# Six places for rows, loads ahead of stores, and later weights in the convolution part of an attention-and-convolution kernel

## The chip, the core and the metric

The kernel runs on one core of one Trainium2 chip. A core has a matrix engine (PE), a vector engine (DVE), a scalar engine (ACT), a general engine (POOL) and a sequencer for transfers and synchronisation (SP). Each runs its own list of instructions in order and waits for others by semaphores. PE reads its operands from the on-chip memory SBUF (128 partitions) and writes to a second on-chip memory, PSUM, from which ACT and DVE take results. Transfers between SBUF and device memory are issued by SP, POOL or ACT as instructions of their own and are carried out by 16 transfer engines that all of these queues share.

The metric is the time of one execution on the device, in microseconds (us); the median of three runs is used.

## What the kernel computes

The reference has two layers on an image batch of 2 x 256 channels x 64 x 64. The first is a full self-attention (8 heads of 32, 4096 positions) whose result is blended with the input by a mask. The second gates the channels, runs attention in 8 x 8 windows, and ends in two grouped 7 x 7 convolutions whose result gates the tensor:

```python
x = _L0_conv_ref(x, mask, Wq, ...)            # attention over all 4096 positions, mask blend
# layer 1
x = x * sigmoid(relu(xp @ ca_w1 + ca_b1) @ ca_w2 + ca_b2)
o = window_attention(x)                        # 8x8 windows, 4 heads of 64
x = x + o @ out_w + out_b
x = shuffle_channels(x, groups=4)
y = conv7x7(x, sa_w1, groups=64); y = relu(bn1(y + sa_b1))
y = conv7x7(y, sa_w2, groups=64); y = bn2(y + sa_b2)
return x * sigmoid(y)
```

All is float32. The change concerns the last three lines.

## The kernel before, in words

**The long part.** `pipeline` walks through 512 slots of the first attention (2 images, 8 chunks of 512 positions, 2 groups of heads, 32 blocks of keys; line 1232). Between the slots it runs the stages of layer 1 for chunks that are done (`stage`, line 766) and issues the transfers that build the convolution weights as band matrices in device memory (`bands`, line 340). The last step of a stage writes the chunk's rows into device memory at `x_s`, with padding (line 1024).

**The convolution part.** `convolve` (line 1038) is a generator. It starts near the end of the slots, runs interleaved with the last stages, and then alone. The 64 channel groups are cut into 16 units of 4 groups (`UG`, `NU`). A 7 x 7 convolution is done as 7 horizontal taps, with a band matrix over image rows for each; three overlapping blocks of rows (`BLOCKS`) cover an image. The work is a list of 26 items of (unit, images) (line 1033), numbered from 0:

- items 0 to 8: units 0 to 8 of image 0 (`EARLY` is 9), whose rows exist before image 1 is done;
- items 9 to 15: units 2 to 8 of image 1;
- items 16 to 21: units 9 to 14, both images at once;
- items 22 to 25: unit 15 of image 0, unit 15 of image 1, units 1 and 0 of image 1.

**One iteration** of the loop at line 1191, for item k: `conv1(k+1)` puts 56 matmuls of the next item on PE, and ACT applies the first activation (line 1102). `conv2(k)` puts 112 matmuls on PE (line 1118); ACT turns the two PSUM tiles into `z` by a tanh (line 1129) and a scaling (line 1135). `gate(k)` multiplies `z` by the rows on DVE (line 1146) and issues 12 stores for each image, four of every twelve on SP and eight on POOL (line 1148), other splits in the last two items. Then `load_rows` issues the load of later rows, and `load_w` that of a later weight, both on SP. All waiting is by semaphores on the tiles. SP, like every engine, goes through its list in order: a load behind a store whose `z` is not ready waits with it.

**Places.** Rows of early items go to four places in one tile, `room` (`early`, line 1042). Later items use four other places, `xcs`, each large enough for two images, made when image 1 is written (`more`, line 1172). Item k + 4 takes the place of item k, so its load is issued in iteration k. `z` has four buffers, one for each image of an item (line 1127). Weights sit in a ring of 8 buffers (`EB`): units 1 to 9 are loaded by iteration 4; from iteration 9 on each iteration loads one more, units 10 to 15 and then unit 1 again (lines 1053 and 1205). Unit 10 takes the buffer that unit 2 leaves with item 9. The first item that reads unit 10 is item 17.

Of the kernel before, what the change touches and what calls it, by code (L numbers as in the profile page):

```python
# [17 lines left out]
B, C, H, W = 2, 256, 64, 64  # L18
# [12 lines left out]
EB = 8  # L31
DN = 8
EARLY = 9
# [4 lines left out]
KS, PAD = 7, 3  # L38
# [19 lines left out]
def conv_seq_kernel(ctx: ExitStack, tc: tile.TileContext, a, out):  # L58
    nc = tc.nc
# [40 lines left out]
    for h in range(HEADS0):  # L100
        n, rows = (0, 32) if h < HG else (1 + (h - HG) // 2, 64)
        p = rows * (h % HG if h < HG else h % 2)
# [271 lines left out]
    with (  # L374
# [50 lines left out]
        for i, (b, c) in enumerate(chunks):  # L425
            load_chunk()
            x = xs0[i]
# [105 lines left out]
    def pipeline(arm, shifted, pools):  # L533
# [499 lines left out]
        items = [(u, (0,)) for u in range(EARLY)] + [(u, (1,)) for u in range(2, EARLY)]  # L1033
# [4 lines left out]
        def convolve():  # L1038
            nb = len(BLOCKS)


            early, xcs, ycs = [], [], []
            room = cpool.tile([P, ROOM], F32, tag="room", name=f"xe{arm}")
            room = room.rearrange("p (k n g w) -> p k n g w", k=4, n=nb, g=UG)
# [6 lines left out]
            xs, ws, ys = {}, {}, {}  # L1051

            weights = deque([*range(1, NU), 1])
            dst = out.rearrange("b (g i) r w -> b i r g w", i=4)

            def load_w(u):
                if u >= NU:
                    return
                n = 2 * 32 * UW
                if u == 0:  # L1060
                    t = cpool.tile([P, n], F32, tag="w0", name=f"w{arm}{u}")
                else:
                    t = ep.tile([P, HG, CH], F32, tag="e", name=f"w{arm}{u}")
                    t = t.rearrange("p h n -> p (h n)")[:, 0:n]
                nc.sync.dma_start(t, w_s[u])
                ws[u] = t

            def load_x(k):
                u, images = items[k]
                x = xs[k] = early[k % 4] if k < EARLY else xcs[k % 4]  # L1070
                for i, b in enumerate(images):
                    nc.sync.dma_start(
                        x[:, nb * i : nb * i + nb].rearrange("p n g w -> p n (g w)"),
                        x_s[b, :, :, UG * u : UG * u + UG, :].rearrange("n p g w -> p n (g w)"),
                    )

            def load_rows(k):

                while len(xs) < min(k + 1, len(items)) and (
                    staged or B - 1 not in items[len(xs)][1]  # L1080
                ):
                    load_x(len(xs))

            def conv1(k):
                if k >= len(items):
                    return
                u, images = items[k]
                n = nb * len(images)
                w = ws[u][:, 0 : 32 * UW].rearrange("p (m g d) -> p g d m", g=UG, d=KS)
                s = psum1(f"c1{arm}{k}")  # L1090
                for d in range(KS):
                    for j in range(4):
                        nc.tensor.matmul(  # L1093
                            s[32 * j : 32 * j + 32, 0 : n * W],
                            w[:, j, d, :],
                            xs[k][:, 0:n, j, d : d + W],
                            start=(d == 0),
                            stop=(d == KS - 1),
                        )
                y = ys[k] = ycs[k % 2]  # L1100
                nc.scalar.activation(
                    y[:, 0:n, PAD : PAD + W],
                    s[:, 0 : n * W].rearrange("p (n x) -> p n x", x=W),
                    AF.Relu,
                    bias=cbias1[:, u : u + 1],
                )

            def conv2(k):
                u, images = items[k]
                n = nb * len(images)  # L1110
                y = ys.pop(k)
                w = ws[u][:, 32 * UW :].rearrange("p (m d) -> p d m", d=KS)
                tiles = [psum2(f"c2{arm}{k}_{hh}") for hh in range(2)]
                for d in range(KS):
                    for j in range(4):
                        r = slice(32 * j, 32 * j + 32)
                        for o in HALVES:
                            nc.tensor.matmul(  # L1118
                                tiles[j // 2][o, j % 2, 0 : n * W],
                                w[r, d, o],  # L1120
                                y[r, 0:n, d : d + W],
                                start=(d == 0),
                                stop=(d == KS - 1),
                            )
                zs = []
                for m in range(len(images)):
                    z = pool.tile([P, 4, nb * W], F32, tag="z", name=f"z{arm}{k}_{m}", bufs=4)
                    for hh in range(2):
                        nc.scalar.activation(  # L1129
                            z[:, 2 * hh : 2 * hh + 2, :],  # L1130
                            tiles[hh][:, :, m * nb * W : (m + 1) * nb * W],
                            AF.Tanh,
                            scale=0.5,
                        )
                    nc.scalar.activation(z, z, AF.Copy, bias=0.25, scale=0.25)  # L1135
                    zs.append(z.rearrange("p j (n x) -> p j n x", x=W))
                while held:
                    held.popleft()()
                return zs

            def gate(k, zs):
                u, images = items[k]
                for m, b in enumerate(images):
                    z = zs[m]
                    x = xs[k][:, nb * m : nb * m + nb, :, PAD : PAD + W]
                    nc.vector.tensor_mul(z, z, x.rearrange("p n g x -> p g n x"))  # L1146

                    engines = (nc.gpsimd, nc.gpsimd, nc.sync)
                    if k == len(items) - 1:
                        engines = (nc.scalar, nc.sync)  # L1150
                    elif k == len(items) - 2:
                        engines = (nc.scalar, nc.sync, nc.sync)
                    stores = 0
                    for n, (x0, r0, r1) in enumerate(BLOCKS):
                        for i in range(4):
                            p = 32 * i + 1 - x0
                            stores += 1
                            args = (
                                dst[b, i, r0:r1, UG * u : UG * u + UG, :],
                                z[p + r0 : p + r1, :, n, :],  # L1160
                            )
                            eng = engines[stores % len(engines)]
                            if eng is nc.scalar:
                                held.append(lambda a=args: nc.scalar.dma_start(*a))
                            else:
                                eng.dma_start(*args)  # L1166
                if k == len(items) - 1:
                    while held:
                        held.popleft()()


            def more():
                if staged and not xcs:

                    for n in range(3):
                        t = ep.tile([P, HG, CH], F32, tag="sum", name=f"xl{arm}{n}", bufs=3)
                        t = t.rearrange("p h n -> p (h n)")[:, 0 : B * nb * UG * WP]
                        xcs.append(t.rearrange("p (n g w) -> p n g w", n=B * nb, g=UG, w=WP))
                    xcs.append(pool.tile([P, B * nb, UG, WP], F32, name=f"xl{arm}3"))
                    load_rows(EARLY)  # L1180
                return bool(xcs)

# [8 lines left out]
            for k, (u, images) in enumerate(items):  # L1191
                while len(xs) <= k + 1 < len(items):
                    if not more():
                        yield
                conv1(k + 1)
                yield
                more()
                z = conv2(k)
                yield
                more()  # L1200
                gate(k, z)
                if xcs or k + 4 < EARLY:
                    load_rows(min(len(xs) + (k >= EARLY - 1), k + 4))

                if weights and (weights[0] <= 1 + EB or k >= EARLY):
                    load_w(weights.popleft())

        def run_later():
# [150 lines left out]
```

## Time and profile before

| | |
|---|---|
| median of 3 runs | 2908.93 us (2906.93 to 2909.06) |
| the profiled execution | 2910.0 us, span 2908.0 us |
| PE busy | 2864.2 us, 98% of the span |
| ACT, DVE, POOL busy | 2455.7, 2435.1, 584.8 us |
| convolution part, last 26 items | from about 2688 us to the end of the span |
| 840 KB of rows for two images (two loads), 420 KB for one | 23 loads of later rows |
| 896 KB for one unit's weights | 17 loads |

A profile line of a group gives the engine, the line of the kernel, the operation, output and input by name, how often, and the busy time. A line of the timeline gives start, duration, engine, line and operation of a run of like instructions, and in brackets how long the engine stood idle ahead of it and what ended that; "issue" there means that nothing the profile records ended it. In a table of windows each engine's busy time and count is given by stretch, then the granted clock of PE as a share, the busy share of the 16 transfer engines, and GB/s.

### The profile page before, as it was taken

To read this page: it belongs to the slowest core of one execution; us is meant where nothing else is said; L and a number is where in the kernel's file an instruction comes from. 1 tells how busy PE (TensorE), PEld (TensorE's weight loads), DVE (VectorE), ACT (ScalarE), POOL (GpSimd) and SP (SyncE) were. 2 spreads that over 40 slices of the span, in tenths; PEclk is the share of its full clock that TensorE was granted. 3 is DMA by queue.
4 is the path that set the end of the run, shared out by engine and by line. 5 is a ranking of instruction groups with operands and counts; after the bars stand their busy time and mean duration, and the time that the engine had idled before them with its cause. 6 is when DMAs were issued, how large, how long until landed. Compare 5 with 4: busy or idle time off the path is not lost.

```text
span 2908.0 us, 85469 instructions
## 1 busy us (share of the span) xinstructions
PE 2864.2 (98%) x37002; PEld 828.2 (28%) x37002; DVE 2435.1 (84%) x1344; ACT 2455.7 (84%) x4145; POOL 584.8 (20%) x965
## 2 busy tenths in 40 slices
PE   9999999999999999999999999999999999999997
PEld 3551122222222222222222222222222222222665
DVE  4249999899999999999989999999999899999211
ACT  5569989898989898989989898989898898989433
POOL 8111111111111212121111111111212110000468
PEclk9999999999999999999999999999999999999999
DMA  8546533333353535353433324343535342242574
GB/s 253 210 162 189 149 86 86 88 83 87 72 95 76 105 80 105 75 95 86 85 93 80 85 70 95 80 98 76 106 79 94 85 85 78 67 115 85 142 221 105
DMA packets 243590, 305.66 MB, mean 105 GB/s; under 512 B 118768, under 2 KB 135348, under 8 KB 242948
## 3 DMA queue, kind: packets, MB, share of 16 engines
q1 hardware_dynamic: 197072, 230.83, 28.7%
q0 software_dynamic: 41360, 66.48, 12.7%
q8 instruction: 293, 4.80, 0.7%
q10 hardware_dynamic: 4772, 2.79, 0.4%
q14 instruction: 93, 0.76, 0.1%
HBM read 221.88 MB, written 66.39 MB: 99 GB/s over the span
## 4 chain that ended last, share of the span: by engine, by line
PE 89%; DMA 4%; POOL 3%; issue 1%; DVE 1%; ACT 1%; ACTq 0%; SPq 0%; DVEq 0%; POOLq 0%
PE sa L643 35%; PE ava L695 33%; PE qka L529 4%; PE hya L529 3%; POOL out_dram L1166 2%; PE vwa L529 2%; PE opa L529 2%; PE v L475 2%; PE q L438 1%; PE k L438 1%; PE c2a L1118 1%; PE c1a L1093 1%; DMA invs<-inva 1%; PE sca L882 1%; DMA folda<-suma 1%
## 5 line engine op out<-in xcount | busy, mean ns | idle before, releaser
L656 ACT ACTIVATE ea<-sa 128x512 f32<-128x512 f32 (+1 forms) x3072 | 2037.0, 746 | 50.1 <-PE sa L643 23.3
L643 PE MATMUL sa<-qa,ka 32*64 32x512 f32 x16384 | 1146.6, 613 | 1.5 <-ACT vst L483 1.2
L701 DVE TENSOR_TENSOR suma<-suma,ea 128x2048 f32<-128x2048 f32 x480 | 1096.2, 2284 | 5.7 <-ACT ea L656 0.5
L695 PE MATMUL ava<-ea,va 128*32 128x512 f32 x8192 | 1091.6, 605 | 1.0
L701 DVE TENSOR_TENSOR odda<-odda,ea 128x2048 f32<-128x2048 f32 x420 | 958.3, 2282 | 46.1 <-ACT ea L656 46.0
L673 POOL DMA_DIRECT2D folda<-suma x336 | 235.5, 891 | 1664.0 <-DVE suma L703 980.0
L643 PEld LDWEIGHTS sa<-qa,ka 32*64 32x64 f32 x16384 | 242.3, 129 | 786.0 <-ACT ea L656 716.9
L695 PEld LDWEIGHTS ava<-ea,va 128*32 128x32 f32 x8192 | 161.4, 108 | 834.2 <-issue 804.7
L1166 POOL DMA_DIRECT2D out_dram<-za x240 | 135.7, 573 | 51.7 <-DVE za L1146 26.6
L701 DVE TENSOR_TENSOR suma<-ea,ea 128x2048 f32<-128x2048 f32 x32 | 73.1, 2286 | 58.8 <-ACT ea L656 58.8
L529 PE MATMUL qka<-ua,qkv_w 128*32 128x512 f32 x1024 | 115.8, 592 | 0.1
L1146 DVE TENSOR_TENSOR za<-za,xla 128x768 f32<-128x768 f32 x23 | 22.1, 959 | 99.3 <-ACT za L1135 46.6
L785 ACT ACTIVATE ta<-hya,bf 128x512 f32<-128x512 f32 x32 | 20.3, 685 | 99.6 <-PE hya L529 93.6
L1024 POOL DMA_DIRECT2D xs<-xo x94 | 72.0, 1037 | 137.2 <-DVE xo L1009 133.3
L457 DVE TENSOR_REDUCE top<-sq 128x128 f32<-128x2048 f32 x16 | 36.6, 2284 | 74.5 <-ACT sq L451 74.5
L741 POOL DMA_DIRECT2D invs<-inva x62 | 34.2, 559 | 297.6 <-DVE inva L756 296.6
L1118 PE MATMUL c2a<-yca,wa 32*64 32x192 f32 (+1 forms) x2912 | 86.3, 368 | 5.5 <-issue 5.1
L903 ACT ACTIVATE ewa<-ewa,mxwa 128x64 f32<-128x64 f32 x256 | 85.4, 346 | 1.5 <-DVE mxwa L894 1.5
L1129 ACT ACTIVATE za<-c2a 128x384 f32<-128x384 f32 x64 | 27.9, 487 | 69.2 <-PE c2a L1118 37.7
L789 DVE TENSOR_TENSOR ta<-ta,mca 128x512 f32<-128x512 f32 x32 | 22.0, 688 | 65.7 <-ACT ta L785 65.7
L1118 PEld LDWEIGHTS c2a<-yca,wa 32*64 32x64 f32 x2912 | 68.1, 191 | 24.5 <-issue 17.3
L861 ACT ACTIVATE qka<-qka,qkv_b 128x512 f32<-128x512 f32 x64 | 40.3, 683 | 39.5 <-PE qka L529 39.5
(143 smaller groups left out, 1714.8 us busy)
## 6 DMA issues: line engine op xcount, KB each, us to landing
ka<-ks SPq DMA_DIRECT2D x256, 256.0 KB
va<-vs SPq DMA_DIRECT2D x256, 256.0 KB
wa<-ws SPq DMA_DIRECT2D x17, 896.0 KB
ws<-zeros SPq DMA_DIRECT2D x16, 896.0 KB
folda<-suma POOLq DMA_DIRECT2D x224, 64.0 KB, 3.1
folda<-suma POOLq DMA_DIRECT2D x112, 128.0 KB, 3.9
xs<-xo POOLq DMA_DIRECT2D x78, 140.0 KB, 7.7
xla<-xs SPq DMA_DIRECT2D x23, 420.0 KB
```

The source lines that it names most:

```text
L438: nc.tensor.matmul(s[:, g, :], w[:, kc, g * P : (g + 1) * P], rhs, start=(kc == 0), stop=(kc == KC - 1),)
L475: nc.tensor.matmul(sv[:, m, :], xs0[i][:, kc, m * P : (m + 1) * P], wv[:, kc, :], start=(kc == 0), stop=(kc == KC - 1),)
L529: nc.tensor.matmul(out[o : o + 32], weights[:, o : o + 32], x, start=start, stop=stop)
L643: nc.tensor.matmul(heads[j][o], k[r, cols][:, o], q[r, g, :], start=True, stop=not shifted)
L656: nc.scalar.activation(e[:, h, :], tile, AF.Exp, scale=SCALE0)
L673: nc.gpsimd.dma_start(dst[p : p + rows], total[rows * k : rows * k + rows, h, :], accum_op=ALU.add if k else ALU.bypass,)
L695: nc.tensor.matmul(av[r, :], v[:, m % PB, r], e[:, j, :], start=start, stop=stop)
L701: nc.vector.tensor_add(total, first.pop(m % chains, total), e)
L903: nc.scalar.activation(e[:, n, :], e[:, n, :], AF.Exp, bias=mx[:, n : n + 1], accum_out=rs[:, n : n + 1],)
L1024: eng.dma_start(x_s[b, n, p + r0 : p + r1].rearrange("r g w -> g r w"), xo[64 * h : 64 * h + 64, oc, r0 - WS * c : r1 - WS * c, :],)
L1118: nc.tensor.matmul(tiles[j // 2][o, j % 2, 0 : n * W], w[r, d, o], y[r, 0:n, d : d + W], start=(d == 0), stop=(d == KS - 1),)
L1166: eng.dma_start(*args)
```

## The change

Five edits in `convolve`:

1. `xcs` gets two more places, both in `room`, the tile of the early rows: first its second half, then its first half. The ring of later rows has six places and starts with item 9 at place 0; item k + 6 takes the place of item k.
2. `gate` is split: `gate(k)` holds only the multiplications of all images of the item, `store(k)` all its stores.
3. Between them stands `load_rows`, so that the loads of iteration k are ahead of its stores in SP's list, and it looks `len(xcs)` items ahead, six in place of four.
4. Stores of items with two images alternate between POOL and SP, 12 and 12 in place of 16 and 8. Item 23 (third from the end) puts 8 of its 12 on SP and 4 on POOL in place of 4 and 8. The last two items' splits are as before.
5. The weights of units 10 to 15 and the second load of unit 1 are loaded from iteration 13 on in place of 9.

```diff
-                x = xs[k] = early[k % 4] if k < EARLY else xcs[k % 4]
+                x = xs[k] = early[k % 4] if k < EARLY else xcs[(k - EARLY) % len(xcs)]
...
             def gate(k, zs):
                 u, images = items[k]
+                for m in range(len(images)):
+                    x = xs[k][:, nb * m : nb * m + nb, :, PAD : PAD + W]
+                    nc.vector.tensor_mul(zs[m], zs[m], x.rearrange("p n g x -> p g n x"))
+
+            def store(k, zs):
+                u, images = items[k]
+                engines = (nc.gpsimd, nc.gpsimd, nc.sync)
+                if k == len(items) - 1:
+                    engines = (nc.scalar, nc.sync)
+                elif k == len(items) - 2:
+                    engines = (nc.scalar, nc.sync, nc.sync)
+                elif k == len(items) - 3:
+                    engines = (nc.gpsimd, nc.sync, nc.sync)
+                elif len(images) == 2:
+                    engines = (nc.gpsimd, nc.sync)
+                stores = 0
                 for m, b in enumerate(images):
-                    z = zs[m]
-                    x = xs[k][:, nb * m : nb * m + nb, :, PAD : PAD + W]
-                    nc.vector.tensor_mul(z, z, x.rearrange("p n g x -> p g n x"))
-
-                    engines = (nc.gpsimd, nc.gpsimd, nc.sync)
-                    if k == len(items) - 1:
-                        engines = (nc.scalar, nc.sync)
-                    elif k == len(items) - 2:
-                        engines = (nc.scalar, nc.sync, nc.sync)
-                    stores = 0
                     for n, (x0, r0, r1) in enumerate(BLOCKS):
...
                     xcs.append(pool.tile([P, B * nb, UG, WP], F32, name=f"xl{arm}3"))
+                    for n in (2, 0):
+                        xcs.append(room[:, n : n + 2].rearrange("p k n g w -> p (k n) g w"))
                     load_rows(EARLY)
...
                 gate(k, z)
-                if xcs or k + 4 < EARLY:
-                    load_rows(min(len(xs) + (k >= EARLY - 1), k + 4))
-
-                if weights and (weights[0] <= 1 + EB or k >= EARLY):
+                if xcs:
+                    load_rows(min(len(xs) + (k >= EARLY - 1), k + len(xcs)))
+                elif k + 4 < EARLY:
+                    load_rows(k + 4)
+                store(k, z)
+
+                if weights and (weights[0] <= 1 + EB or k >= EARLY + 4):
                     load_w(weights.popleft())
```

More of the change, by code (lines that the diff above doesn't have):

```diff
@@ L1159, in gate @@
                                 dst[b, i, r0:r1, UG * u : UG * u + UG, :],
-                                z[p + r0 : p + r1, :, n, :],
+                                zs[m][p + r0 : p + r1, :, n, :],
                             )
```

## The prediction

> **What bounds the kernel now.** I read the page first, for the engine that sets the whole; then a table of windows over the convolution part, which alone is changed; then the timelines of PE and SP there, and POOL's at the end.
>
> ```profile
> PE 2864.2 (98%) x37002; PEld 828.2 (28%) x37002; DVE 2435.1 (84%) x1344; ACT 2455.7 (84%) x4145; POOL 584.8 (20%) x965
> ...
> q8 instruction: 293, 4.80, 0.7%
> ```
>
> PE bounds the whole. Its 74,004 matmuls and weight loads over the 293 transfers of the instruction queue are 253 apiece: this queue feeds PE its instructions, 4.80 MB / 293 = 16 KB at a time.
>
> ```profile
> 2762.00:2808.00 46.00, 40.86 (x1203) 33.81 (x1202) 6.71 (x7) 15.23 (x29) 32.79 (x59) 0.96 0.73 210
> 2808.00:2866.00 58.00, 57.99 (x1124) 33.70 (x1114) 9.59 (x10) 20.53 (x38) 44.99 (x81) 1.00 0.66 185
> 2866.00:2893.00 27.00, 25.50 (x784) 21.45 (x780) 6.71 (x7) 13.70 (x27) 26.51 (x48) 1.00 0.44 94
> ```
>
> The columns are the stretch, its length, busy time of PE, PE's weight loads, DVE, ACT and POOL, granted clock, transfer share, GB/s. PE idles 5.1 us in the one-image items (first row), nothing in the two-image items, 1.5 us in the last items. POOL is full at the end, with stores only.
>
> ```profile
> 2781.99 0.76 PE L1118 MATMUL c2a<-yca,wa 32*64 32x192 f32 x17 [1.17 <-issue]
> ...
> 2788.30 1.60 PE L1118 MATMUL c2a<-yca,wa 32*64 32x192 f32 x58 [1.56 <-issue]
> ...
> 2802.97 0.63 PE L1118 MATMUL c2a<-yca,wa 32*64 32x192 f32 x11 [2.18 <-issue]
> 2803.53 4.19 PE L1093 MATMUL c1a<-xla,wa 128*32 128x192 f32 x56
> ...
> 2884.39 2.54 PE L1093 MATMUL c1a<-xla,wa 128*32 128x192 f32 x56 [0.84 <-DMA xla<-xs]
> ```
>
> The large stalls are in the middle of a `conv2`, wait for no data, and end 2.3 to 2.4 us after a 16 KB transfer of the instruction queue starts (2779.58, 2786.01 and 2800.72 in the transfer records): PE waits for its own instructions. After the third, PE runs at half clock from about 2803 to 2807 and the next `conv1` takes 4.19 us in place of 2.5. The last line is the only stall on rows.
>
> ```profile
> 2785.45 2.25 SPq L1166 DMA_DIRECT2D out_dram<-za  x4
> 2787.75 0.38 SPq L1072 DMA_DIRECT2D xla<-xs  x1
> 2788.23 0.43 SPq L1065 DMA_DIRECT2D wa<-ws  x1
> ...
> 2868.71 4.19 SPq L1166 DMA_DIRECT2D out_dram<-za  x8
> ...
> 2879.83 1.42 SPq L1072 DMA_DIRECT2D xla<-xs  x1
> 2881.35 20.73 SPq L1166 DMA_DIRECT2D out_dram<-za  x22
> ```
>
> SP issues rows and a weight together, behind the stores. In the transfer records rows for one image take some 24 pieces of 60 ns on each engine, 1.4 us, a weight 8 pieces of 285 ns, 2.3 us. The last row load is issued at 2879.83 and used at 2884.39.
>
> [...] The trace shows 0.50 after 2.18 us and a row of shorter stalls.
>
> **The ideal and what is lost.** Unstalled durations in the timeline are 2.47 and 2.57 us for conv1 and conv2 of one image, 4.76 and 4.81 of two. From conv2(7), 2762.3, to the last matmul at 2892.6 are 130.3 us. Needed: conv1(9 to 25) 7 x 2.47 + 6 x 4.76 + 4 x 2.47 = 55.7; conv2(7 to 25) 9 x 2.57 + 6 x 4.81 + 4 x 2.57 = 62.3; 118.0 in all. Lost: 12.3. By place: conv2(7, 8) 0.6; conv2(10) to conv2(14) 1.6 + 2.1 + 0.5 + 0.4 + 2.7 + 1.7 + 0.6 = 9.6, of which the half clock is 2.2; the last items 1.9, with the late row's 0.84. After the last matmul come tanh, scaling, product, 24 stores by SP and ACT, landing: 15.4 us to the span's end.
>
> **The change, part by part.**
>
> *Two places, look-ahead of six.* No instruction is added. Item 25's rows are issued in iteration 19 in place of 21, about 17 us earlier: the 0.84 us wait goes, and row traffic leaves the last items. I take 1.0 us. Other rows were never awaited, so their earlier coming gives nothing itself. The places in `room` are free: item 13's needs item 6's product, item 14's needs item 8's, the last instruction before it.
>
> *Loads ahead of stores.* The loads pass the stores on SP only; POOL's list keeps its order. In items 0 to 4 too they wait for the same product as the stores did, so they come 1.6 us earlier and meet nothing new. A one-image store set waits behind 1 or 2 loads, 0.4 to 0.9 us on SP. Hidden: `z` returns four images later, some 20 us in one-image items, 16.5 us after the product in two-image ones; POOL's 12 x 0.57 = 6.8 us plus 3.5 us to land is 10.3. If it were not, ACT's tanh would wait, then PSUM, then PE. For two-image items all stores now wait for the second product, 1.6 us more, covered by the same slack.
>
> *Stores from POOL to SP.* Six items move 4 each, item 23 moves 4: 28 x 0.573 = 16.0 us off POOL, which ended at 2896.9, not last. On SP 28 x 0.50 (six runs of 8 in the two-image items: 24.2 us / 48) = 14.1 us more. In a two-image iteration SP then has 12 x 0.50 + a load 0.4 + a weight 0.4 = 6.8 of 9.57 us: room. At the end: items 20 to 25 have 12, 12, 4, 8, 8, 6 stores = 50 x 0.50 = 25 us from 2870.3, so SP is at leisure again before item 24's product (2892.2). I take 0.
>
> *Weights four iterations later.* The four weights of iterations 9 to 12, 4 x 2.3 = 9.2 us of transfer time, leave the one-image items; weights 10 and 11 are still issued there (iterations 13, 14), but most of their data moves under conv1(16) and conv1(17), which run at 4.76 us per 112 instructions and so need a block half as often. Against it, rows come denser: two loads in each of iterations 8 and 10 to 14. Transfer need per 5.0 us: 2 x 1.4 rows + 1.3 stores (0.30 share over 4.4 us per image near the end) = 4.1, where rows plus weight plus stores were 5.0 to 6.4. So the saturated stretch becomes a busy one[...]. Rows-only iterations before (items 9 to 11) cost 0.2, 0.35, 0 and once 1.6: mean 0.5 per iteration. Pairs of rows: bounded by 0.3 below (no worse than one) and 1.1 above (twice that mean); I take 0.7. After: iterations 5 to 9 five times 0.6 = 3.0, 10 to 13 four times 0.7 = 2.8, the half clock at a chance of one in seven 0.3: 6.1 in place of 0.6 + 9.6 = 10.2. Gain 4.1; at the bounds, nine times 0.3 or 1.1, it is 7.5 or 0.3.
>
> *Is weight 10 in time?* From iteration 13's product to conv1(17) are conv2(13)'s end + 2.47 + 2.57 + 4.76 + 2.57 = 12.4, less 2.8 to the product's end: 9.5 us. Two loads 0.9, four stores 1.7, and 5.2 to 6.9 us from issue to the last piece (weights of 2747 and 2809): 7.8 to 9.5, with 0.4 for the signal 8.2 to 9.9. I take 0 and keep a loss of 0.5 in the range. Weight 11 has 14 us.
>
> Sum: 4.1 + 1.0 = 5.1 us. The profiled execution's 2910.0 would become 2904.9; it stands 1.1 above the median, so 2908.9 - 5.1 = 2903.8.
>
> **Rivals.** *(B) Nearly all stalls go*, since without weights a fetch is never late enough, and the clock stays whole: 10.2 - 1.0 left + 1.0 late row = 10 us, 2899 (2897 to 2901). For: the two longest stalls have a weight in flight. Against: the 1.17 us stall at 2781 began before any. *(C) Paired rows stall PE as weights did*: gain -1 to 2.5, 2906.4 to 2910. For: the row bytes moved forward nearly equal the weight bytes moved back. Against: pieces a fifth as long. *(D) Slower: SP becomes the last queue.* Its 50 stores from 2870.3 would end later than 2902.1 once one costs over 0.64 us; beyond 0.2% of loss from about 0.75 us, at some 2915 to 2920. For: the last 14 took 9.84 us, 0.70 each. Against: 0.50 in the runs of 8, and gaps between products there. That the change doesn't take effect is no rival I can see: six places change the place of every item.
>
> **How the numbers follow.** 0.2% is 5.8 us, about what a measurement of this kernel can tell from no change: bounds 2903.1 and 2914.7. Main case 0.50, 2901.3 to 2906.4, of which 0.19 below 2903.1; B 0.22, C 0.20, D 0.08. Faster 0.19 + 0.22 = 0.41; same 0.31 + 0.20 = 0.51; slower 0.08. The range 2898.3 to 2910.0 leaves out D, some of B (0.07) and a little of C.
>
> **What would show it.** Right: conv2(11) to conv2(13) with stalls under 1 us, PE's clock 1.00 from 2762 to 2866, transfer share more even (near 0.75 in both), no idle on rows at conv1(25), POOL done before 2893, SP's tail about as before. Wrong: a stall at conv1(17) on weights; half clock again; SP's stores of item 21 still running when item 24's product is done; ACT's tanh waiting for stores while PE stands.

## The result

The changed kernel takes 2907.37 us, median of 22 runs, where the kernel before takes 2912.26 us, median of 22: a ratio of 0.9984, 95% interval 0.9978 to 0.9991, that is 4.7 us saved (2.6 to 6.4). Measured a second time, 2904.83 against 2909.95: 0.9981 (0.9973 to 0.9988), 5.5 us. The prediction was 5.1 us saved, with a change of under 0.2% as the likeliest outcome. The sum was right; the experiments show that its terms were not.

First a caution on how the two profiles compare. The profiled execution of the changed kernel took 2911.2 us with a span of 2909.3 us, more than the one shown of before (2910.0 and 2908.0). Up to the first `conv1` the two kernels run the same list, yet it starts at 2689.7 us in one and 2687.5 in the other, and anywhere from 2684.5 to 2693.3 us over the 14 profiles of this study. Whole spans of single executions can't show 5 us. So each profile is read by pieces, cut by PE's matmuls:

- A: from the first matmul of conv1(0) to the start of conv2(7), interleaved with the last stages;
- B: from the start of conv2(7) to the last matmul, 118.0 us without any stall;
- C: from the last matmul to the end of the span.

| | A | B | C |
|---|---|---|---|
| before, two profiles | 74.8, 77.2 | 130.3, 128.5 | 15.4, 15.6 |
| changed, two profiles | 79.4, 78.1 | 126.0, 125.9 | 14.2, 14.2 |

In the mean B is 3.5 us and C 1.3 us shorter, and A is 2.8 us longer. The pieces together give 2.0 us and not the 4.7 to 5.5 us of the medians. Two profiles of each kernel don't settle A, so the saving is taken from the medians and the pieces only say where to look.

The convolution part of the changed kernel by windows, cut where its one-image, two-image and last items stand (columns: stretch, length, busy PE, its weight loads, DVE, ACT, POOL, PE's clock, transfer share, GB/s):

```profile
2769.10:2814.50 45.40, 40.80 (x1292) 35.04 (x1289) 6.71 (x7) 15.42 (x29) 33.06 (x60) 1.00 0.64 173
2814.50:2869.60 55.10, 55.10 (x1017) 31.71 (x1015) 9.59 (x10) 20.25 (x36) 37.43 (x68) 1.00 0.77 228
2869.60:2895.20 25.60, 25.24 (x787) 21.28 (x784) 6.71 (x7) 13.57 (x26) 21.41 (x38) 1.00 0.49 107
```

Traffic has moved from the one-image to the two-image items (share 0.73 and 0.66 before, 0.64 and 0.77 now), the clock is whole, POOL is no longer full at the end, and PE idles 0.4 us in the last items where it idled 1.5. But PE still idles 4.6 us in the one-image items.

So little of what B gained is idle time in the one-image items. From conv2(7) to conv2(17) PE idles 5.2 and 4.9 us in the two profiles of before, and 4.6 and 5.0 us in those of the changed kernel. What is gone is one spell of 3.4 us at half clock in each profile of before, from 2803.9 and 2804.2 us, which costs up to 1.7 us (the `conv1` in it took 4.19 and 3.79 us in place of 2.5), and 0.8 us of idle time behind conv2(17). PE's stalls in the changed kernel, from the timeline:

```profile
2777.29 1.66 PE L1118 MATMUL c2a<-yca,wa 32*64 32x192 f32 x64 [1.50 <-issue]
...
2798.82 2.56 PE L1118 MATMUL c2a<-yca,wa 32*64 32x192 f32 x98 [1.05 <-issue]
...
2804.05 1.52 PE L1093 MATMUL c1a<-xea,wa 128*32 128x192 f32 x27 [1.19 <-issue]
...
2808.89 0.63 PE L1118 MATMUL c2a<-yca,wa 32*64 32x192 f32 x11 [0.82 <-issue]
```

The count at the end of each line is what was left of the group when PE resumed. From 98 left of conv2(12) to 27 left of conv1(14) are 98 + 29 = 127 matmuls, each with its weight load: 254 instructions. From there to 11 left of conv2(13): 27 + 101 = 128 matmuls, 256 instructions. One 16 KB transfer of the instruction queue brings 253 on average, here as before. So these stalls sit about one such transfer apart, as those of before did, whose 17, 58 and 11 matmuls left come again in other kernels below. In the transfer records of the changed kernel such transfers start at 2774.84, 2796.29, 2801.80 and 2806.45 us, and each of the four stalls ends 2.2 to 2.5 us after one. From this the stalls are read as waits of PE for its own instructions; what differs between kernels is how long they are, and whether PE runs at half clock afterwards.

SP and POOL in the changed kernel:

```profile
2812.34 0.91 SPq L1072 DMA_DIRECT2D xea<-xs  x2
2813.35 1.72 SPq L1172 DMA_DIRECT2D out_dram<-za  x4
2815.11 0.36 SPq L1065 DMA_DIRECT2D wa<-ws  x1
...
2853.87 6.13 SPq L1172 DMA_DIRECT2D out_dram<-za  x12
```

```profile
2879.20 15.18 POOL L1172 DMA_DIRECT2D out_dram<-za  x27 [1.41 <-issue]
```

Rows now go first, then four stores, then a weight, which is unit 10's here, issued 2.8 us after the rows. A set of twelve stores takes SP 6.1 us of a 9.6 us iteration.

### The profile page after: what moved, and what is told of

It is laid out like the page before. It is cut to its first block, busy times and chain, and to the rows that moved or that the text cites. A ratio compares the mean times of both kernels' runs of the same rounds, so it can differ in the third digit from the quotient of the medians.

```text
span 2909.3 us, 85471 instructions
## 1 busy us (share of the span) xinstructions
PE 2863.8 (98%) x37002; PEld 827.4 (28%) x37002; DVE 2435.4 (84%) x1344; ACT 2455.3 (84%) x4145; POOL 569.1 (20%) x937
## 4 chain that ended last, share of the span: by engine, by line
PE 89%; DMA 4%; POOL 2%; issue 2%; DVE 2%; ACT 1%; ACTq 0%; POOLq 0%; DVEq 0%
PE sa L643 34%; PE ava L695 33%; PE qka L529 4%; PE hya L529 3%; PE c1a L1093 2%; PE vwa L529 2%; PE opa L529 2%; PE c2a L1118 2%; PE v L475 2%; PE q L438 2%; PE k L438 1%; DMA xs<-xo 1%; POOL out_dram L1172 1%; DMA invs<-inva 1%; DMA folda<-suma 1%
## 5 line engine op out<-in xcount | busy, mean ns | idle before, releaser
L1172 POOL DMA_DIRECT2D out_dram<-za x212 | 119.7, 573 | 58.7 <-DVE za L1145 31.8
L457 DVE TENSOR_REDUCE top<-sq 128x128 f32<-128x2048 f32 x16 | 36.6, 2285 | 74.8 <-ACT sq L451 74.8
L1145 DVE TENSOR_TENSOR za<-za,xla 128x768 f32<-128x768 f32 x16 | 15.3, 959 | 65.2 <-DMA out_dram<-za 36.4
```

## The experiments

All ratios are to the kernel before on the same chip in the same session.

| kernel | ratio (95% interval) | A | B | C |
|---|---|---|---|---|
| changed, again | 0.9981 (0.9973 to 0.9988) | 78.1 | 125.9 | 14.2 |
| late weights alone | 1.0001 (0.9992 to 1.0009) | 77.5 | 128.2 | 15.2 |
| changed, weights put back | 0.9984 (0.9977 to 0.9991) | 77.8 | 126.6 | 14.4 |
| before, later weights left out | 0.9989 (0.9981 to 0.9997) | 76.2 | 126.8 | 14.8 |
| changed, store split put back | 0.9988 (0.9982 to 0.9995) | 80.0 | 126.0 | 15.9 |
| late weights and new split | 0.9994 (0.9985 to 1.0002) | 77.6 | 125.0 | 14.1 |
| six places alone | 1.0003 (0.9995 to 1.0011) | 76.7 | 130.5 | 15.3 |
| loads in front alone | 0.9991 (0.9983 to 0.9999) | 77.5 | 125.4 | 16.6 |
| the same, weight in front too | 1.0010 (1.0003 to 1.0018) | 75.0 | 129.7 | 15.3 |
| changed, early loads put back | 0.9978 (0.9970 to 0.9987) | 74.3 | 125.2 | 14.5 |
| the same with four places | 0.9976 (0.9969 to 0.9983) | 76.9 | 124.8 | 14.6 |

**Do the profiles repeat?** The changed kernel and the kernel before, run again.

> The changed kernel as it is, once more, for a second profile of it. From the start of conv2(7) to the end of the last matmul the first profile of it has 126.0 us where the kernel before has 130.3 and 118.0 are needed without a stall. If the stalls belong to the order of the transfers, this stretch comes again at 125 to 127 us, with no stall on rows at conv1(25) and no half clock after iteration 12, and the time stays 3 to 7 us under the kernel before. If they fall as chance has it, the stretch moves by 3 us or more. The same for the stall of 3.35 us in conv1(6), ahead of the stretch, which the kernel before has at 1.66: if the loads ahead of the early stores make it, it comes again at over 2.5 us.

> The kernel before once more, for a second profile of it: its stretch from conv2(7) to the last matmul again at 129 to 131.5 us (130.3 in the first) with 15.4 us to the end, if the order of the transfers makes the stalls; conv1(0) to conv2(7), 74.8 us in the first and lowest of all, nearer to 76.6.

B came again at 125.9 us for the changed kernel. For the kernel before it came at 128.5, under the 129 expected: about 2 us of B is chance, and a difference of 3 us or more in one profile is what may be read. C repeats within 0.2 us. A of before was 77.2 the second time: the 74.8 of the first was low. In conv1(6), in A, the stall was 2.92 us in the changed kernel's second profile and 2.90 us in the second of before. It doesn't tell the two apart.

**Late weights alone** (`w_only`).

```diff
-                if weights and (weights[0] <= 1 + EB or k >= EARLY):
+                if weights and (weights[0] <= 1 + EB or k >= EARLY + 4):
```

> The kernel before with one edit of the change alone: the weights from iteration 13 on in place of 9. Theory (weights in the one-image items hold up PE's instruction fetches): most of the gain is here, 3 to 5 us, conv2(11) to conv2(13) lose under 2 us together where they lost 5.4, and the 0.8 us wait for rows at conv1(25) stays. Rival (the gain is of the deeper look-ahead or of the store split): 0 to 1 us, the stalls of conv2(11) to conv2(13) stay above 4 us.

The loss from conv2(7) to conv2(14), stalls and half clock together, fell to 5.1 us from 10.6 (8.5 in the second profile of before), so the weights do bear on these stalls. But the time did not move, and B only to 128.2. PE, ACT and POOL at item 22 show a new wait:

```profile
2877.90 4.10 PE L1118 MATMUL c2a<-yca,wa 32*64 32x192 f32 x104 [2.47 <-ACT za L1129]
```

```profile
2872.46 0.87 ACT L1129 ACTIVATE za<-c2a 128x384 f32<-128x384 f32 x2 [3.39 <-DMA out_dram<-za]
2873.36 0.85 ACT L1135 ACTIVATE za<-za 128x768 f32<-128x768 f32 x1
2877.36 0.87 ACT L1129 ACTIVATE za<-c2a 128x384 f32<-128x384 f32 x2 [3.14 <-DMA out_dram<-za]
```

```profile
2868.89 31.57 POOL L1166 DMA_DIRECT2D out_dram<-za  x56 [1.18 <-DVE za L1146]
```

ACT waits for a `z` buffer whose stores haven't landed, PE waits for the PSUM tile that ACT holds, conv2(22) takes 4.5 us too long, part of it at half clock (the clock is 0.60 in the mean from 2878 to 2882 us). POOL has 56 stores in a row to issue. What was gained on those stalls was lost on `z`.

**The changed kernel with its weights put back** (`w_back`; the same line, reversed).

> The changed kernel with that one edit undone: six places, loads ahead of stores and the new split, but the weights from iteration 9 on. Theory: pairs of rows and weights meet in iterations 10 to 12, the stretch from conv2(7) to the last matmul is 130 us or more, the time is that of the kernel before within 2 us, or slower. Rival (deeper look-ahead or split): the gain stays at 3 to 6 us.

The theory fell here: the gain stays, 0.9984, and B is 126.6 us where 130 or more was expected. The late weights are not what carries the change.

**No later weights at all** (`no_weights`): units 10 to 15 and the second load of unit 1 take unit 9's weights without a transfer.

```diff
+                if u > 1 + EB or u in ws:
+                    ws[u] = ws[1 + EB]
+                    return
```

> The kernel before with the transfers of the weights of units 10 to 15 and of the second load of unit 1 left out; those items multiply by unit 9's weights in their place, so the output of these units isn't the reference's, while all matmuls, rows and stores stay. It prices the weights' share of all stalls. Theory: the stretch from conv2(7) to the last matmul loses 2 to 5 us over the 118.0 needed, of it 0.8 at conv1(25), and the time is 6 to 9 us under the kernel before. Rival (rows and stores alone hold up the fetches): the stretch still loses 8 us or more, the time falls by under 4 us.

The rival came true on both counts: 3.2 us (0.9 to 5.5) are saved, and B still loses 8.8 us with rows and stores alone. The later weights cost some 3 us in all, and no placing of them alone can be expected to win much more than that.

**The old store split in the changed kernel** (`stores_back`: 16 and 8 for two images, 8 and 4 for item 23).

> The changed kernel with the old split of the stores: 16 on POOL and 8 on SP for items with two images, 8 and 4 for item 23. Revised theory, from the run with the weights alone: late weights crowd the transfer engines in the two-image items, POOL's list of stores falls behind, buffers of z come back late, ACT's tanh of item 21 waits for them and PE for ACT's PSUM tile. Then PE stalls 2 to 5 us between conv2(20) and conv2(23) with ACT waiting on stores, POOL's last store is issued after 2895 us, and the gain shrinks to 0 to 2 us. Rival, as the prediction had it (the split is worth nothing): the time is that of the changed kernel within 1.5 us, no PE stall there.

The theory was wrong: B is 126.0 us with no wait for `z`, so the stall of `w_only` doesn't come back here, and why it doesn't stays open. The rival had PE right. But 3.5 us are saved here and 4.7 and 5.5 in the changed kernel; the intervals meet, so the times alone don't tell the two apart. The pieces do: C is 15.9 where the new split has 14.2. Over all 14 profiles C is 14.1 to 14.6 us with the new split (six) and 14.8 to 16.6 with the old one (eight). The end of the instruction records tells why. There each engine has a drain, an instruction behind its last one. With the old split POOL, after its last store, spends 7.2 to 7.3 us in this drain in every one of the eight profiles, and it ends 0.86 us before the span does, last of all; ACT's drain was over 0.7 to 2.6 us before POOL's (in `stores_back` it ended 3.27 us before the span's end). With the new split POOL's stores end earlier and ACT's drain is the last, at 0.84 us before the end; POOL's was done 7.0 to 10.5 us before the end in all six. POOL's last stores of the kernel before and of this one:

```profile
2895.69 1.17 POOL L1166 DMA_DIRECT2D out_dram<-za  x2
```

```profile
2867.38 31.57 POOL L1168 DMA_DIRECT2D out_dram<-za  x56 [0.88 <-issue]
```

The drains of POOL before and in the changed kernel (shortest, median and longest in ns, then the first and last start in us); the longest is the first, behind the stores:

```profile
L1355 POOLq DRAIN  x3: 50/113/7217, 2899.9 to 2907.7; - x3
```

```profile
L1365 POOLq DRAIN  x3: 50/113/4868, 2896.0 to 2909.0; - x3
```

Before, POOL's drain runs from 2899.94 to 2907.16 of 2908.0. The split is worth what C shows, 1.2 us in the mean of these profiles; where it is the only edit between two kernels, 15.2 against 14.1 us (`w_only`, `w_split`) and 15.9 against 14.2 (`stores_back`, changed).

**Late weights and new split together** (`w_split`): two edits of the change on the kernel before.

> The kernel before with two of the edits: weights from iteration 13 on and the new split of the stores. Four places, loads behind the stores. Theory: the fetch stalls stay as low as with the weights alone (about 5 us from conv2(7) on), the 4.5 us stall at conv2(22) is gone, rows for conv1(24) and conv1(25) cost 1 to 3 us; the stretch from conv2(7) to the last matmul is 124 to 126 us and the time 3 to 5 us under the kernel before. Rival (places and order of loads make the gain): 0 to 1.5 us.

The profile is nearly as expected: B is 125.0 us, 2.9 us are lost up to conv1(16), 0.6 of it in a wait for ACT, and 3.1 us at conv1(24) and conv1(25), where PE waits for ACT and for rows. The time is not: 0.9994, and the interval includes 1. One profile was kinder than the median.

**Six places alone** (`six_only`).

> The kernel before with six places and a look-ahead of six alone: loads behind the stores, weights from iteration 9, old split. It tells whether the early rows are what carries the changed kernel with its weights put back, which kept the whole gain. If the places do it: the rows stall of 0.8 to 1.2 us at the end is gone, conv2(10) and conv2(11) lose under 1 us together, the time is 2 to 4 us under the kernel before. If the order of the loads or the split does it: within 1.5 us of the kernel before, fetch stalls of 8 us or more.

No gain, 1.0003. The wait for rows at the end is gone, as in the changed kernel, but conv2(7) to conv2(14) lose 12 us. Three of its stalls, and SP's order at the last:

```profile
2784.88 0.76 PE L1118 MATMUL c2a<-yca,wa 32*64 32x192 f32 x17 [1.42 <-issue]
2791.18 1.60 PE L1118 MATMUL c2a<-yca,wa 32*64 32x192 f32 x58 [1.55 <-issue]
...
2806.95 0.94 PE L1118 MATMUL c2a<-yca,wa 32*64 32x192 f32 x11 [3.00 <-issue]
```

```profile
2802.97 1.06 SPq L1072 DMA_DIRECT2D xla<-xs  x2
2804.13 1.84 SPq L1065 DMA_DIRECT2D wa<-ws  x1
```

**Loads in front of stores alone** (`front_only`): `gate` and `store` split, `load_rows` between them; four places, weights from iteration 9, old split. The cut shows the order; the conditions on `load_rows` are left out, and the loads of early rows move too.

```diff
                 gate(k, z)
-                if xcs or k + 4 < EARLY:
-                    load_rows(...)
+                load_rows(...)
+                store(k, z)
                 if weights and (weights[0] <= 1 + EB or k >= EARLY):
```

> The kernel before with the loads of rows in front of the stores alone: four places, weights from iteration 9, old split. A row load then has its stores between it and the weight, some 1.7 us of issuing, in place of standing against it. If the back-to-back pair of row and weight is what holds up PE's fetches: the stalls from conv2(10) to conv1(15) fall from 9.0 to under 5 us and the time by 2 to 4 us. If not: the stalls stay at 7 us or more and the time within 1.5 us of the kernel before.

This edit, which the prediction priced at nothing, has B at 125.4 us by itself. conv2(10) to conv1(15) lose 3.1 us, where they lost 9.0 and 7.8 in the two profiles of before; the clock stays whole there (1.00 from 2763.9 to 2812 us). The time falls by 2.6 us (0.3 to 4.9), close to the 3.2 us that leaving the later weights out saves. PE's two longest stalls from conv2(10) on:

```profile
2796.22 1.53 PE L1093 MATMUL c1a<-xla,wa 128*32 128x192 f32 x27 [0.92 <-issue]
...
2806.82 1.58 PE L1118 MATMUL c2a<-yca,wa 32*64 32x192 f32 x51 [1.67 <-issue]
```

**The weight in front as well** (`w_adjacent`): the same kernel, with the weight from iteration 9 on ahead of the stores too.

```diff
                 load_rows(...)
+                if weights and k >= EARLY:
+                    load_w(weights.popleft())
                 store(k, z)
-                if weights and (weights[0] <= 1 + EB or k >= EARLY):
+                if weights and weights[0] <= 1 + EB and k < EARLY:
```

> The kernel with the loads in front of the stores alone, and from iteration 9 on the weight in front of them too, right behind the rows: rows, weight, stores, where front_only has rows, stores, weight and the kernel before stores, rows, weight. Theory (the back-to-back pair of rows and weight holds up PE's fetches): the stretch from conv2(7) to the last matmul goes back to 128 us or more from 125.4, and the time to within 1.5 us of the kernel before. Rival (rows in front help because they come earlier against PE's list, whatever stands behind them): 124 to 127 us, the time 2 to 4 us under the kernel before.

B went back to 129.7 us, as the theory has it. The time went further than expected, to 2.9 us above the kernel before (0.9 to 5.2). SP's order in `front_only` and then in `w_adjacent`, and PE's two long stalls in the latter:

```profile
2785.74 0.38 SPq L1072 DMA_DIRECT2D xla<-xs  x1
2786.21 1.71 SPq L1168 DMA_DIRECT2D out_dram<-za  x4
2788.02 0.36 SPq L1065 DMA_DIRECT2D wa<-ws  x1
```

```profile
2782.21 0.39 SPq L1072 DMA_DIRECT2D xla<-xs  x1
2782.70 0.42 SPq L1065 DMA_DIRECT2D wa<-ws  x1
2783.22 2.76 SPq L1168 DMA_DIRECT2D out_dram<-za  x4
```

```profile
2785.25 2.15 PE L1118 MATMUL c2a<-yca,wa 32*64 32x192 f32 x58 [1.81 <-issue]
...
2805.39 1.78 PE L1118 MATMUL c2a<-yca,wa 32*64 32x192 f32 x51 [1.93 <-issue]
2807.11 6.22 PE L1093 MATMUL c1a<-xla,wa 128*32 128x384 f32 x56
```

The stretch of these stalls by windows, `front_only` and then `w_adjacent`; PE's clock is the third number from the end:

```profile
2763.90:2812.00 48.10, 44.25 (x1337) 36.82 (x1338) 7.67 (x8) 17.16 (x32) 36.60 (x66) 1.00 0.82 238
```

```profile
2757.00:2808.00 51.00, 46.13 (x1352) 37.75 (x1348) 7.67 (x8) 18.32 (x35) 38.52 (x69) 0.95 0.75 221
```

The weight is issued 2.3 us after its rows in the first and 0.5 us after in the second. B is 4.3 us longer in the second, and the intervals of the two times don't meet. Idle time makes 0.9 us of the 4.3: from conv2(7) to conv2(17) PE idles 3.9 us in `front_only` and 4.8 in `w_adjacent`. Most of the rest is half clock: each of the two stalls shown for `w_adjacent` is followed by a spell of 3.4 us, and `front_only` has none. The second makes conv1(16) take 6.22 us in place of 4.8. By the measure used above, conv2(10) to conv1(15) lose 4.9 us here, against 3.1 in `front_only` and 7.8 and 9.0 before: in this profile the loss is only partly back in the same place.

The rows have the same place in SP's list in both kernels and the bytes are the same, so neither explains the difference. From before to `front_only` the weight keeps its place behind rows and stores and only the rows move; from `front_only` to `w_adjacent` only the weight moves. The distance of rows and weight in SP's queue changes in both steps, and it is the one cause that explains both. What is not excluded is that each step has a cause of its own, since in `w_adjacent` the weight also comes 1.8 us earlier. The other kernels agree with the distance: the six with rows ahead of the stores and weights behind them have ratios of 0.9976 to 0.9991, and the four others that load later weights, where rows and weight stand together, 0.9994 to 1.0010. How the pair would hold up a fetch was not shown.

**Early loads put back** (`early_back`): in the changed kernel the loads of items 0 to 4's iterations stand behind their stores again.

```diff
-                elif k + 4 < EARLY:
-                    load_rows(k + 4)
                 store(k, z)
+                if not xcs and k + 4 < EARLY:
+                    load_rows(k + 4)
```

> The changed kernel with the loads of early rows (items 0 to 4) behind the stores again, all else as changed. In five profiles with early loads behind the stores conv1(0) to conv2(7) took 74.8 to 77.6 us, mean 76.6; in five with them ahead 77.5 to 80.0, mean 78.6. If that order makes the 2.0 us: this piece takes under 77.6 us here and the time falls to 5 to 8 us under the kernel before. If the difference is chance, or comes from what follows the end of the stages: 77.5 us or more, and the time of the changed kernel within 1.5 us.

A is 74.3 us and the time 0.9978. Its stall in conv1(6), and that of the changed kernel:

```profile
2744.48 2.36 PE L1093 MATMUL c1a<-xea,wa 128*32 128x192 f32 x50 [1.81 <-issue]
```

```profile
2750.45 3.75 PE L1093 MATMUL c1a<-xea,wa 128*32 128x192 f32 x50 [3.35 <-issue]
```

Over all profiles A is 74.3 to 77.6 us with early loads behind the stores (eight, mean 76.4) and 75.0 to 80.0 with them ahead (six, mean 78.0). The means differ by 1.6 us, but the ranges overlap, and so do the intervals of the two times. That the edit costs something in the early items is likely and not shown.

**The same with four places** (`four_places`): the two places in `room` left out of `early_back`.

> The same without the two further places: four places and a look-ahead of four, later rows ahead of the stores, weights from iteration 13 on, the new split, early loads behind the stores. If the two places are worth nothing, as alone, this is at least as fast as the changed kernel: stretch from conv2(7) to the last matmul 122 to 126 us, 14.2 us from there to the end, time 5 to 9 us under the kernel before, the best of all. If the places are needed once the weights come late: conv1(24) or conv1(25) waits for rows 1.5 us or more, the stretch is 126 us or more.

As fast without them: 0.9976 (0.9969 to 0.9983), 7 us under the kernel before. It is faster than the kernel before beyond doubt. Against the changed kernel its ratio is lower by 0.0005 to 0.0008, with intervals that meet, so that part is not settled.

## Why the prediction was right, and where its steps were not

*The bound and the stalls*: right. PE's idle time in the one-image items is mainly in stalls that sit 254 to 256 instructions apart; the three that the prediction shows of before and the four shown of the changed kernel end 2.2 to 2.5 us after a transfer of the instruction queue starts. After the change 8.0 us of B are lost where 12.3 - 5.1 = 7.2 were forecast. But the stalls there did not shrink as a whole, as the idle times above show: the half clock behind the longest of them went.

*"Weights four iterations later"*, with a gain of 4.1: the size is that of a real effect, in the wrong place. Alone, the edit takes 3.4 to 5.5 us of loss away up to conv2(14), by the two profiles of before, and the time stays; taken out of the changed kernel, the time stays too. The estimate counted bytes per iteration. By the experiments what most probably counts is the pair of rows and weight in the queue (`w_adjacent` has it and a B of 129.7 us, `front_only` has not and 125.4), and the next step breaks that pair as well. Probably the two edits remove the same loss, and so they don't add.

*"Loads ahead of stores"*, priced by what they delay, at nothing: this is the failed step. It looked at who waits behind a load, and not at what the reordering puts between rows and weight. In B the edit alone is worth 3 to 5 us by the two profiles of before.

*"Stores from POOL to SP"*, taken as 0: wrong by about 1.2 us. "POOL, which ended at 2896.9, not last" took the last store for the end; the drain behind it ended at 2907.2, last of all. That SP has room was right: twelve stores took 6.0 to 7.4 us, and rival D didn't come.

*"Two places"*, taken as 1.0: the wait for rows at conv1(25) is gone, as forecast, but the places alone bring nothing. `front_only` and `four_places` have no such wait either, with four places: loads ahead of the stores are enough for it.

*The cover of `z`*: "hidden" held in the changed kernel, where no PE stall comes from it. In `w_only` it failed, with 4.5 us.

*Weight 10 in time*: right; conv1(17) starts without a gap in every profile with late weights. *The half clock*: gone in B of the changed kernel, as forecast, still there at conv1(6), where 50 matmuls took 3.75 us after a stall of 3.35.

*The early items, "meet nothing new"*: open, with up to 1.6 us against it in the means.

The total came right by luck: 4.1 us were booked to one edit that another edit earns, 1.0 us to places that earn nothing alone, and 1.2 us at the end and what the early items may cost, both not booked, have opposite signs.

## What to carry to other kernels

When an engine stalls for no reason that the profile gives, at places a fixed number of instructions apart (254 to 256 here), look at what stands in the transfer queues then: here a load of 896 KB right behind one of 420 KB went with 4.9 us lost from conv2(10) to conv1(15), and four stores of 16 or 24 KB between them with 3.1 us, for the same bytes. Read the clock together with the idle time, because a stall can cost nearly as much again in the clock behind it: 2.18 us of stall and up to 1.7 us of half clock before. Two edits that cure the same stall must be priced together, and each also alone. The end of an engine here was the end of its drain, not its last store: 2907.16 against 2896.86 us for POOL before.

## What the hardware showed beyond that

POOL's drain at the end took 7.2 to 7.3 us in all eight profiles in which POOL was issuing stores until 10 to 12 us before the span's end, and 4.8 to 6.3 us in the six with the new split, where its last store was issued 15 to 18 us before the end.

In B of the 14 profiles there are seven stalls of 1.8 us or more, 1.81 to 3.29 us, and each was followed, within 1.7 us of its end, by a spell of 3.4 us at half clock. No stall of up to 1.67 us was. In A this is not so sharp: at conv1(6) a stall of 1.81 us (`early_back`) and one of 3.03 us (`w_adjacent`) had no such spell behind them.

The same list of instructions ahead of the convolution part ended within a spread of 8.8 us over 14 single executions, 2684.5 to 2693.3 us. That is more than any effect studied here, and the reason to read pieces and medians.
